# Four graph layers in one kernel: layernorm per block, and each layer's projections placed inside its first output block

## The chip, the cores and the metric

The kernel runs on one core of one Trainium2 chip. The metric is the device time of one execution in microseconds. Before the change three executions took 3187.55, 3188.2 and 3189.6 us; the median is 3188.2. The profiled execution has a span of 3186.7 us. Lower is better.

## The reference

There are N = 4096 nodes with D = 256 features, and a 0/1 matrix `adj` of 4096 x 4096 with ones on its diagonal. Four layers follow one another; each adds its result to the features and normalises every row to mean 0 and variance 1 (layernorm). So layer n+1 needs the normalised rows of layer n.

```python
x = _layernorm(x + _L0_gnn_ref(x, adj, W, a))          # additive attention, 4 heads of 64
x = _layernorm(x + _L1_gnn_ref(x, adj, Wq, bq, ...))   # multi-head attention, 4 heads of 64
x = _layernorm(x + _L2_gnn_ref(x, adj, W, a))          # additive attention, one head of 256
x = _layernorm(x + _L3_gnn_ref(x, adj, Wq, Wk))        # attention by cosines, 128 wide
```

- Layers 0 and 2: `Wh = x @ W`; the score of target i and source j is `leaky_relu(s_i + s_j)`, where both terms are products of `Wh` with a vector; where `adj` is 0 the weight is 0; softmax over the sources j; the output is the weighted sum of `Wh`, through `elu`.
- Layer 1: `q`, `k`, `v` are `x @ W + b`; the scores `q . k / 8` get a mask that takes away entries without an edge; softmax; weighted sum of `v`.
- Layer 3: `q` and `k` are `x @ Wq.T` and `x @ Wk.T`, with each row scaled to length 1; the score is their product; masked softmax; the result is `0.5 * (weighted sum of x) + 0.5 * x`. For a node with no neighbour at all the sum is replaced by x itself.

## The kernel before, in words

Rows are held in 32 tiles of 128 rows (`NT`); four of them (`QB`) make a block of 512 rows, so there are 8 blocks (`NB`). The features stay in one SBUF tensor `X` for the whole kernel, with a column of ones behind the 256 features.

Each layer has the same shape:

1. *A prologue over the 8 blocks.* `transposed_block` turns a block's tiles on TensorE (L92) and copies them to SBUF, one half on VectorE and one on ScalarE (L94 to L96). Then the projections: `additive_values` for layers 0 and 2 (L145, with three small exponentials on ScalarE and one multiply on VectorE for each tile, L147 to L152), keys, queries and values for layer 1 (L347 to L358), rows and their lengths for layer 3 (L496 to L507). Layer 1 then takes a maximum over all keys and queries for its shift (L361 to L374). Layer 3 takes a square root over all lengths, scales the rows (L513), turns them and copies them into `T` (L515 to L518). PSUM tiles of the prologue come in two buffers for each name.
2. *A loop over output blocks b and source tiles j.* `weights(b, j)` makes the masked, unnormalised softmax weights of 128 sources and 512 targets: an activation on ScalarE (L209, L402, L283, L536), then a multiply by the mask on VectorE (L210, L405, L285, L537). Masks are loaded in pieces through SyncE's queue, in layer 3 through GpSimd's. `sums(b, j)` adds the weighted features in PSUM on TensorE (L219 and L223, L425, L291, L544). `sums` is issued one step behind `weights` (two in layer 3). Layer 1 also makes its scores on TensorE (L400) and adds its denominators on GpSimd and by accumulating DMAs (L412, L418); its weights have 8 buffers.
3. *Outputs of block b - 1*, placed a few steps into block b: division by the denominator, `elu` in layers 0 and 2, the addition to `X`, and the mean and variance of each row (`row_stats`, L99).
4. *After the loop*, the outputs of the last block, and `layernorm` over all 32 tiles: one square root on ScalarE (L105), one reciprocal (L106) and 32 subtract-and-multiply operations on VectorE (L109). In layer 3 the results go to the DRAM in eight stores (L580).

In layer 0 the target term of each block must lie along the free dimension of all 128 partitions. `rows(b)` does this with one transpose and a way through DRAM (L192 to L200).

The code is written for a framework with a scheduler. It gives each engine one queue in an order of its own, from the order of the statements and from its idea of what is ready; an engine then works through its queue in order, and waits on semaphores. A buffer of a pool can be used again when its last readers have signalled. A pool that is opened where another was closed waits for the work in the old one.

Of the kernel before, what the change touches and what calls it, by code (L numbers as in the profile page):

```python
# [26 lines left out]
def kernel(  # L27
# [24 lines left out]

    nc = tc.nc
# [3 lines left out]

    const = ctx.enter_context(tc.tile_pool(name="const", bufs=1))
    feat = ctx.enter_context(tc.tile_pool(name="feat", bufs=1))

    ident = const.tile([P, P], FP, name="ident")
    make_identity(nc, ident)
    eps = const.tile([P, 1], FP, name="eps")
    nc.vector.memset(eps, EPS)


    X = feat.tile([P, NT, D + 1], FP, name="X")
    xv = x.rearrange("(t p) d -> p t d", p=P)
    for b in range(NB):
        nc.sync.dma_start(X[:, b * QB:(b + 1) * QB, :D], xv[:, b * QB:(b + 1) * QB, :])  # L70
    nc.vector.memset(X[:, :, D:], 1.0)
    stats = feat.tile([P, NT, 2], FP, name="stats")
    rstd = feat.tile([P, NT], FP, name="rstd")

    def load_w(pool, w, name):
        sb = pool.tile([P, KC, w.shape[1]], FP, name=name)
        nc.scalar.dma_start(sb, w.rearrange("(c p) f -> p c f", p=P))
        return sb

    def spread(pool, ap, dims, shape, name):  # L80

        sb = pool.tile(shape, FP, name=name)
        nc.scalar.dma_start(sb, bass.AP(tensor=ap.tensor, offset=ap.offset, ap=[[0, P]] + dims))
        return sb

    def transposed_block(sb, ps, b):

        xT = sb.tile([P, KC, QW], FP, name="xT")
        for c in range(KC):
            pt = ps.tile([P, QB, P], FP, name="px")  # L90
            for k in range(QB):
                nc.tensor.transpose(pt[:, k, :], X[:, b * QB + k, c * P:(c + 1) * P], ident)  # L92
            if c % 2:
                nc.scalar.copy(xT[:, c, :], pt.rearrange("p k i -> p (k i)"))  # L94
            else:
                nc.vector.tensor_copy(xT[:, c, :], pt.rearrange("p k i -> p (k i)"))  # L96
        return xT

    def row_stats(sb, y, t):  # L99
        st = sb.tile([P, 6], FP, name="bn")  # L100
        nc.vector.bn_stats(st, y)  # L101
        nc.vector.bn_aggr(stats[:, t, :], st)

    def finish_stats():
        nc.scalar.activation(rstd, stats[:, :, 1], AF.Sqrt, bias=eps)  # L105
        nc.vector.reciprocal(rstd, rstd)  # L106

    def normalise(y, t):
        nc.vector.tensor_scalar(y, y, stats[:, t, 0:1], rstd[:, t:t + 1], OP.subtract, OP.mult)  # L109

    def layernorm():
        finish_stats()
        for t in range(NT):
            normalise(X[:, t, :D], t)

# [4 lines left out]
    def additive_values(keep, w, a_src, a_dst, H, slope):  # L120

        d = D // H
        g = 1.0 - slope
        V = keep.tile([P, NT, D + H], FP, name="V")
        src = keep.tile([P, NT, H], FP, name="src")
        dst = keep.tile([P, NT, H], FP, name="dst")
        with tc.tile_pool(name="ga_w", bufs=1) as wp, \
             tc.tile_pool(name="ga_in", bufs=2) as sb, \
             tc.tile_pool(name="ga_ps", bufs=2, space=PSUM) as ps:
            w_sb = wp.tile([P, KC, D + 2 * H], FP, name="w_sb")  # L130
            nc.scalar.dma_start(w_sb[:, :, :D], w.rearrange("(c p) f -> p c f", p=P))
            for n, vec in enumerate((a_src, a_dst)):
                a_sb = spread(wp, *vec, [P, H, d], f"a{n}")
                for c in range(KC):
                    prod = sb.tile([P, H, d], FP, name="prod")
                    nc.vector.tensor_tensor(prod, w_sb[:, c, :D].rearrange("p (h d) -> p h d", h=H), a_sb, OP.mult)
                    lo = D + n * H
                    nc.vector.tensor_reduce(w_sb[:, c, lo:lo + H], prod, AX.X, OP.add)
            for b in range(NB):
                xT = transposed_block(sb, ps, b)  # L140
                for k in range(QB):
                    t = b * QB + k
                    pw = ps.tile([P, D + 2 * H], FP, name="pw")
                    for c in range(KC):
                        nc.tensor.matmul(pw, xT[:, c, k * P:(k + 1) * P], w_sb[:, c, :],  # L145
                                         start=(c == 0), stop=(c == KC - 1))
                    nc.scalar.activation(src[:, t, :], pw[:, D:D + H], AF.Exp, scale=g)  # L147
                    nc.scalar.activation(dst[:, t, :], pw[:, D + H:], AF.Exp, scale=g)
                    nc.scalar.activation(V[:, t, D:], pw[:, D + H:], AF.Exp, scale=slope)
                    nc.vector.tensor_tensor(V[:, t, :D].rearrange("p (h d) -> p h d", h=H),  # L150
                                            pw[:, :D].rearrange("p (h d) -> p h d", h=H),
                                            V[:, t, D:].unsqueeze(2).to_broadcast([P, H, d]), OP.mult)  # L152
        return V, src, dst

    def add_elu(sb, po, rden, t, H):

        o = sb.tile([P, D], FP, name="o")
        heads = "p (h d) -> p h d"
        nc.vector.tensor_tensor(o.rearrange(heads, h=H), po.rearrange(heads, h=H),
                                rden.unsqueeze(2).to_broadcast([P, H, D // H]), OP.mult)  # L160

        neg = sb.tile([P, D], FP, name="neg")
        nc.vector.tensor_scalar_min(neg, o, 0.0)
        nc.scalar.activation(neg, neg, AF.Exp)
        nc.vector.scalar_tensor_tensor(o, neg, -1.0, o, OP.add, OP.max)
        nc.vector.tensor_tensor(X[:, t, :D], X[:, t, :D], o, OP.add)
        row_stats(sb, X[:, t, :D], t)

    def additive_heads(w, a_src, a_dst, H, slope):
# [5 lines left out]
        MJ = 4  # L175
        with ExitStack() as lay:
            keep = lay.enter_context(tc.tile_pool(name="ga_keep", bufs=1))
            V, src, dst = additive_values(keep, w, a_src, a_dst, H, slope)
            rp = lay.enter_context(tc.tile_pool(name="ga_row", bufs=2))
            zp = lay.enter_context(tc.tile_pool(name="ga_z", bufs=5))  # L180
            sb = lay.enter_context(tc.tile_pool(name="ga_sb", bufs=2))
            mp = lay.enter_context(tc.tile_pool(name="ga_mask", bufs=3))
            dr = lay.enter_context(tc.tile_pool(name="ga_dram", bufs=2, space=bass.MemoryType.DRAM))
            ps = lay.enter_context(tc.tile_pool(name="ga_pr", bufs=1, space=PSUM))
            pa = lay.enter_context(tc.tile_pool(name="ga_pa", bufs=2, space=PSUM))
            edges = adjT.rearrange("(t p) i -> p t i", p=P)
            row, mask, acc, prob, kept = {}, {}, {}, {}, {}

            def rows(b):

                pr = ps.tile([QB * H, P], FP, name="pr")
                nc.tensor.transpose(pr, src[:, b * QB:(b + 1) * QB, :].rearrange("p k h -> p (k h)"), ident)  # L192
                line = sb.tile([QB * H, P], FP, name="line")
                nc.scalar.copy(line, pr)
# [18 lines left out]
            def sums(b, js):  # L213
# [11 lines left out]
                if js[-1] == NT - 1:  # L225
                    kept[b] = sb.tile([P, HC + 1, QW], FP, name="kept")
                    for c in range(HC + 1):
                        (nc.vector.tensor_copy if c == 1 else nc.scalar.copy)(kept[b][:, c, :], acc[b][:, c, :])

            def outputs(b, k):  # L230
                po = ps.tile([P, HC + 1, P], FP, name="po")
                for c in range(HC + 1):
                    nc.tensor.transpose(po[:, c, :], kept[b][:, c, k * P:(k + 1) * P], ident)
                rden = sb.tile([P, H], FP, name="rden")
                nc.vector.reciprocal(rden, po[:, HC, ::G])
                add_elu(sb, po[:, :HC, :].rearrange("p c f -> p (c f)"), rden, b * QB + k, H)

            rows(0)
            pairs = [(b, (j, j + 1)) for b in range(NB) for j in range(0, NT, 2)]
            for i in range(len(pairs) + 1):  # L240
                if i < len(pairs):
# [3 lines left out]
                    if js[0] == 2 and b + 1 < NB:  # L245
                        rows(b + 1)
                if i:
                    b, js = pairs[i - 1]
                    sums(b, js)
                    if b and js[0] % 6 == 2 and js[0] // 6 < QB:  # L250
                        outputs(b - 1, js[0] // 6)
            for k in range(QB):
                outputs(NB - 1, k)
            layernorm()

    def additive_one(w, a_src, a_dst, slope):

        MJ = 4
        with ExitStack() as lay:
            keep = lay.enter_context(tc.tile_pool(name="gb_keep", bufs=1))  # L260
            V, src, dst = additive_values(keep, w, a_src, a_dst, 1, slope)
            zp = lay.enter_context(tc.tile_pool(name="gb_z", bufs=3))
            sb = lay.enter_context(tc.tile_pool(name="gb_sb", bufs=2))
            mp = lay.enter_context(tc.tile_pool(name="gb_mask", bufs=3))
            edges = adjT.rearrange("(t p) i -> p t i", p=P)
            row = keep.tile([P, N], FP, name="row")
# [355 lines left out]
```

## Time and profile before

| engine | busy us | share of 3186.7 us |
|---|---|---|
| TensorE (matmul) | 3061.1 | 96% |
| VectorE | 1901.7 | 60% |
| ScalarE | 1661.7 | 52% |
| GpSimd | 825.6 | 26% |

The first product of each loop tells the stages apart: layer 0's loop starts at 72 us, layer 1's at 904, layer 2's at 1963 and layer 3's at 2503; the last products of the loops end at about 783, 1884, 2407 and 3164. A busy TensorE is not a TensorE at its peak, since matmuls are pipelined and their ends modelled; so the distance between repeated instructions is used as well as the busy time. The profile has eight loads of ScalarE's function tables, at 1283 ns each.

### The profile page before, as it was taken

How to read it: one execution, taken by the hardware profiler on the slowest of the kernel's cores; microseconds unless marked ns; L12 is line 12 of the kernel's file. 1: busy time of each engine (PE TensorE's matmuls, PEld its weight loads, DVE VectorE, ACT ScalarE, POOL GpSimd, SP SyncE). 2: the span in 40 equal slices, each digit the busy share in tenths (PEclk: the TensorE clock that was granted, in tenths of full speed). 3: DMA queues.
4: the chain of work that ended last, by engine and by line, in shares of the span. 5: the costliest groups of instructions: out<-in, count | busy, mean ns of one | idle time of the engine just before them, and what ended most of it. 6: DMA issues, size and time to landing. Idle time of an engine off the chain costs nothing. (4 is left out here: it accounts for less than half of the span.)

```text
span 3186.7 us, 37692 instructions
## 1 busy us (share of the span) xinstructions
PE 3061.1 (96%) x14220; PEld 1581.0 (50%) x14220; DVE 1901.7 (60%) x2594; ACT 1661.7 (52%) x2581; POOL 825.6 (26%) x534
## 2 busy tenths in 40 slices
PE   6999999998899999999999979999997999999997
PEld 4222222222543333333333327888886677777775
DVE  3899999998456666666666663454545333333333
ACT  3999999997245555555555543444443322222221
POOL 0000000000048878778778750000000000000000
PEclk9999999999999999999999989999998999999998
DMA  3323333321059989889889871444440433333331
GB/s 126 119 93 106 106 106 110 116 94 60 12 119 218 198 201 215 200 202 216 200 201 217 200 176 53 146 158 146 157 147 4 67 53 47 47 53 53 53 53 53
DMA packets 186263, 390.61 MB, mean 123 GB/s; under 512 B 10721, under 2 KB 53985, under 8 KB 185057
## 3 DMA queue, kind: packets, MB, share of 16 engines
q0 software_dynamic: 67840, 159.40, 27.5%
q1 hardware_dynamic: 114560, 226.58, 22.1%
q10 hardware_dynamic: 3680, 2.23, 0.2%
q8 instruction: 111, 1.82, 0.2%
q14 instruction: 72, 0.58, 0.1%
HBM read 283.25 MB, written 4.26 MB: 90 GB/s over the span
## 5 line engine op out<-in xcount | busy, mean ns | idle before, releaser
L405 DVE TENSOR_TENSOR prob<-p,mask 128x1024 f32<-128x1024 f32 x512 | 596.0, 1218 | 332.7 <-ACT p L402 249.0
L402 ACT ACTIVATE p<-p,shift 128x1024 f32<-128x1024 f32 x512 | 529.3, 1087 | 405.4 <-PE p L400 405.0
L209 ACT ACTIVATE prob<-row,dst 128x512 f32<-128x512 f32 x1024 | 645.4, 712 | 52.1 <-PE acc L223 47.3
L412 POOL TENSOR_TENSOR den<-den,prob 128x1024 f32<-128x1024 f32 x248 | 614.4, 2477 | 132.1 <-DVE prob L405 119.3
L210 DVE SCALAR_TENSOR_TENSOR prob<-prob,mask 128x2048 f32<-128x2048 f32 x256 | 586.5, 2291 | 73.8 <-ACT prob L209 69.1
L400 PE MATMUL p<-qT,kT 64*128 64x512 f32 x2048 | 496.3, 609 | 3.4 <-DVE prob L405 3.0
L544 PE MATMUL acc<-X,prob 128*128 128x257 f32 x2048 | 486.4, 381 | 3.5 <-DVE prob L537 3.5
L425 PE MATMUL acc<-prob,V 128*64 128x512 f32 x2048 | 480.2, 601 | 0.0
L219 PE MATMUL acc<-prob,V 128*64 128x512 f32 x2048 | 469.9, 601 | 8.3 <-DVE prob L210 8.3
L544 PEld LDWEIGHTS acc<-X,prob 128*128 128x128 f32 x2048 | 389.0, 191 | 164.9 <-issue 112.4
L291 PE MATMUL acc<-V,prob 128*128 128x257 f32 x2048 | 444.4, 380 | 0.9 <-ACT row L273 0.9
L537 DVE TENSOR_TENSOR prob<-prob,mask 128x512 f32<-128x512 f32 x256 | 176.3, 691 | 435.9 <-ACT prob L536 426.4
L536 ACT ACTIVATE prob<-p 128x512 f32<-128x512 f32 x256 | 152.4, 598 | 512.0 <-PE p L533 464.4
L291 PEld LDWEIGHTS acc<-V,prob 128*128 128x128 f32 x2048 | 388.6, 190 | 56.6 <-ACT row L273 1.2
L400 PEld LDWEIGHTS p<-qT,kT 64*128 64x128 f32 x2048 | 185.6, 187 | 309.1 <-DVE prob L405 168.3
L531 POOL DMA_DIRECT2D mask<-in_adjT x32 | 28.1, 880 | 1188.2 <-ACT kT L518 611.0
L283 ACT ACTIVATE e<-row,dst 128x512 f32<-128x512 f32 x256 | 185.2, 724 | 244.1 <-DVE prob L285 222.4
L285 DVE SCALAR_TENSOR_TENSOR prob<-e,mask 128x512 f32<-128x512 f32 x256 | 176.9, 691 | 222.3 <-PE acc L291 214.1
L219 PEld LDWEIGHTS acc<-prob,V 128*64 128x64 f32 x2048 | 136.2, 137 | 315.1 <-issue 222.6
L425 PEld LDWEIGHTS acc<-prob,V 128*64 128x64 f32 x2048 | 130.5, 136 | 324.1 <-issue 313.5
L533 PE MATMUL p<-kT,qT 128*128 128x512 f32 x512 | 259.6, 592 | 0.7 <-ACT kT L518 0.7
L223 PE MATMUL acc<-prob,V 128*32 128x512 f32 x2048 | 246.1, 598 | 0.0
(114 smaller groups left out, 1516.5 us busy)
## 6 DMA issues: line engine op xcount, KB each, us to landing
mask<-in_adjT SPq DMA_DIRECT2D x128, 1024.0 KB
den<-prob POOLq DMA_DIRECT2D x240, 512.0 KB, 5.7
mask<-in_adj SPq DMA_DIRECT2D x128, 512.0 KB
mask<-in_adjT POOLq DMA_DIRECT2D x32, 1024.0 KB, 8.2
row<-far SPq DMA_DIRECT2D x8, 1024.0 KB
den<-prob SPq DMA_DIRECT2D x16, 512.0 KB
X<-in_x SPq DMA_DIRECT2D x8, 512.0 KB
out<-Y SPq DMA_DIRECT2D x8, 512.0 KB
```

Of the source, the lines that this page charges most:

```text
L209: nc.scalar.activation(z[:, h, :], row[b][:, h, :], AF.Relu, bias=-1.0, scale=dst[:, j, h:h + 1])
L210: nc.vector.scalar_tensor_tensor(z, z, 1.0, mask[m][:, j % MJ, :].unsqueeze(1).to_broadcast([P, H, QW]), OP.add, OP.mult)
L219: nc.tensor.matmul(acc[b][lo:lo + d, h // 2, :], V[:, j, h * d:(h + 1) * d], prob[b, j][:, h, :], start=(j == 0), stop=(j == NT - 1))
L223: nc.tensor.matmul(acc[b][h * G:(h + 1) * G, HC, :], V[:, j, D + h:D + h + 1].to_broadcast([P, G]), prob[b, j][:, h, :], start=(j == 0), s ...
L291: nc.tensor.matmul(acc[b][k], prob[b, j][:, k * P:(k + 1) * P], V[:, j, :], start=(j == 0), stop=(j == NT - 1))
L400: nc.tensor.matmul(p[:, r, :], kT[half, c, j * P:(j + 1) * P], qT[half, c, cols], start=True, stop=True)
L402: nc.scalar.activation(p, p, AF.Exp, bias=shift)
L405: nc.vector.tensor_tensor(z, p, mask[m][:, j % MJ, :].unsqueeze(1).to_broadcast([P, KC, QW]), OP.mult)
L412: nc.gpsimd.tensor_tensor(to, to, flat, OP.add)
L425: nc.tensor.matmul(acc[b][r * d:(r + 1) * d, c, :], V[:, j, h * d:(h + 1) * d], prob[b, j, c][:, r, :], start=(j == 0), stop=(j == NT - 1))
L533: nc.tensor.matmul(p, T["q"][:, j * P:(j + 1) * P], T["k"][:, cols], start=True, stop=True)
L544: nc.tensor.matmul(acc[b][k], prob[u][:, k * P:(k + 1) * P], X[:, j, :], start=(j == 0), stop=(j == NT - 1))
```

## The change

The change is for the stretches between the loops, where a layer waits for the one before it.

- **Layernorm by block.** When the fourth tile of a block has its mean and variance, the block is normalised at once (`layernorm_block`), inside the loop. The inverse root is now `exp(-0.5 * ln(v))` with one Newton step on VectorE (`inverse_root`), in place of a square root and a reciprocal.
- **Projections inside the first block.** In layers 0, 2 and 3 a function `prepare(b)` does the transposes and projections of one block. Blocks 0 and 1 go ahead of the loop; blocks 2 to 7 are placed among the products of output block 0, one for each four source tiles. Layer 0's first row comes from 16 transposes of a broadcast column in place of the way through DRAM. Layer 3 makes its projections of queries and keys in one product of 256 columns, and its inverse lengths by `inverse_root` for each block.
- **The last block inside the next layer.** `additive_heads` and `multi_head_attention` return a function `tail`, which the next layer calls: layer 1 behind the keys of its block 0, layer 2 ahead of its loop. Layer 2's last outputs stand ahead of layer 3's `prepare(0)`.
- **Buffers.** PSUM tiles of all these are 512-column banks from one shared pool (`bank`): eight in layer 1's prologue, two in layer 0, four in layer 2 (shared with the sums of odd blocks), two in layer 3 (shared with the scores of later blocks). All pools release by tile. Layer 1's weights have 7 buffers instead of 8. The weights of layers 0, 1 and 2 are loaded at the start.
- **Layer 3's outputs** leave out the case of a node without neighbours (no row lacks its diagonal), and are stored by block.

```diff
+    def inverse_root(v, n):
+        r = fin.tile([P, n], FP, name=f"r{n}")
+        nc.scalar.activation(r, v, AF.Ln)
+        nc.scalar.activation(r, r, AF.Exp, scale=-0.5)
...
+        nc.vector.tensor_tensor(s, r, r, OP.mult)
+        nc.vector.tensor_tensor(s, s, v, OP.mult)
+        nc.vector.tensor_scalar(s, s, -0.5, 1.5, OP.mult, OP.add)
+        nc.vector.tensor_tensor(r, r, s, OP.mult)
+        return r
...
+    def normalise(ys, mv):
...
+        nc.vector.tensor_scalar_add(v, mv[:, :, 1], EPS)
+        r = inverse_root(v, n)
+        for k, y in enumerate(ys):
+            nc.vector.tensor_scalar(y, y, mv[:, k, 0:1], r[:, k:k + 1], OP.subtract, OP.mult)
...
-            rows(0)
+            prepare(0)
+            first_rows()
+            prepare(1)
...
+                    if b == 0 and js[0] % QB == 2 and js[0] // QB + 2 < NB:
+                        prepare(js[0] // QB + 2)
...
-            for k in range(QB):
-                outputs(NB - 1, k)
-            layernorm()
...
+        def tail(bank):
             for k in range(QB):
-                outputs(NB - 1, k)
-            layernorm()
+                outputs(bank, NB - 1, k)
+        return tail
...
-                 tc.tile_pool(name="mh_ps", bufs=2, space=PSUM) as ps:
+                ps = pool(pro, "mh_ps", 8, space=PSUM)
...
+                keys(0)
+                tail(bank)
+                values(0)
...
-            zp = lay.enter_context(tc.tile_pool(name="mh_z", bufs=8))
+            zp = pool(lay, "mh_z", 7)
...
-                nc.scalar.activation(norm, norm, AF.Sqrt)
-                nc.vector.tensor_scalar_max(norm, norm, 1e-4)
-                nc.vector.reciprocal(norm, norm)
...
+                nc.vector.tensor_scalar_max(v, norm.rearrange("p k n -> p (k n)"), 1e-8)
+                r = inverse_root(v, QB * 2)
+                flat = rows.rearrange("p k n f -> p (k n) f")
+                nc.vector.tensor_tensor(flat, flat, r.unsqueeze(2).to_broadcast([P, QB * 2, P]), OP.mult)
...
+            prepare(0)
+            prepare(1)
             units = [(b, j) for b in range(NB) for j in range(NT)]
...
+                    if b == 0 and j % QB == 2 and j // QB + 2 < NB:
+                        prepare(j // QB + 2)
```

## The prediction

> **What bounds the kernel now.** I read, in this order, the busy time by stage (windows I cut where the traced layers change), the chain of work that ended last, the costliest groups, and the instructions in order of time around the seams. Columns of the first view: window, its length, then busy us (and instructions) of TensorE (PE), its weight loads (PEld), VectorE (DVE), ScalarE (ACT) and GpSimd (POOL), then granted clock, DMA share, GB/s.
>
> ```profile
> 0.00:72.00 72.00, 44.26 (x199) 32.79 (x199) 23.64 (x51) 21.64 (x118) 0.70 (x6) 0.94 0.41 139
> 72.00:783.00 711.00, 711.00 (x4175) 198.30 (x4179) 640.11 (x458) 653.49 (x1063) 0.00 (x0) 1.00 0.32 102
> 783.00:904.00 121.00, 101.40 (x351) 58.36 (x340) 59.13 (x139) 31.18 (x48) 0.00 (x0) 0.92 0.03 9
> 904.00:1884.00 980.00, 976.08 (x4266) 328.08 (x4266) 628.50 (x595) 543.14 (x535) 796.79 (x496) 1.00 0.91 204
> 1884.00:1963.00 79.00, 51.88 (x248) 37.25 (x246) 38.26 (x95) 24.13 (x121) 0.00 (x0) 0.85 0.17 52
> 1963.00:2407.00 444.00, 443.95 (x2047) 388.56 (x2048) 222.08 (x453) 192.18 (x281) 0.00 (x0) 1.00 0.46 145
> 2407.00:2503.00 96.00, 71.26 (x399) 53.71 (x398) 54.60 (x198) 43.75 (x163) 2.70 (x3) 0.88 0.10 15
> 2503.00:3164.00 661.00, 661.00 (x2548) 483.93 (x2548) 219.04 (x544) 151.86 (x254) 25.43 (x29) 1.00 0.32 49
> 3164.00:3186.70 22.70, 0.24 (x2) 0.00 (x0) 16.31 (x66) 0.32 (x1) 0.00 (x0) 0.61 0.56 185
> ```
>
> The four loops (711, 980, 444, 661 us) are TensorE's; the five seams between and around them sum to 72 + 121 + 79 + 96 + 22.7 = 391 us, of which TensorE works 269. Only the seams can shrink, and their matrix work does not vanish: it moves into a loop that TensorE already bounds.
>
> The chain says the same:
>
> ```profile
> 1963.05 443.09 PE acc L291 x2042
> 2414.70 6.61 DVE X L109 x21
> ...
> 2497.53 4.70 issue
> ...
> 3170.42 6.87 DVE Y L109 x21
> ```
>
> Layer 2's loop is one unbroken run of products; around it, the normalisation of all 32 tiles (L109) and a wait for the first mask (4.7 us) are bare time.
>
> Layer 0's loop matters for added work, because there the other engines are nearly full too:
>
> ```profile
> L209 ACT ACTIVATE prob<-row,dst 128x512 f32<-128x512 f32 x1024 | 645.4, 712 | 52.1 <-PE acc L223 47.3
> L210 DVE SCALAR_TENSOR_TENSOR prob<-prob,mask 128x2048 f32<-128x2048 f32 x256 | 586.5, 2291 | 73.8 <-ACT prob L209 69.1
> ```
>
> A pair of source tiles takes 5.44 us on TensorE (products start at 433.61, the next pair's transposes at 439.04). ScalarE needs 8 x 645.4/1024 = 5.04 us of it, VectorE 2 x 2.29 = 4.58.
>
> **What the Trainium skill says.** "ScalarE: Activation LUTs", section "What ACT_TABLE_LOAD costs": a switch of table set is about 1283 ns plus a drain of about 1380 ns. The trace agrees with the first and shows no drain of that size:
>
> ```profile
> 2493.40 0.59 ACT L518 COPY kT<-px 128x512 f32<-128x512 f32 x1 [0.20 <-PE px L517]
> 2494.01 1.28 ACT L536 ACT_TABLE_LOAD   x1
> 2495.30 0.60 ACT L536 ACTIVATE prob<-p 128x512 f32<-128x512 f32 x1
> ```
>
> The load starts 0.02 us after the copy ends, and the exponential starts as it ends, so I take 1.28. Same page, section "Table sets: the hidden batching unit": Ln and Exp share one set and need one load. The instruction order of the built program disagrees for this change: it has a load before each Ln and another before the Exp after it, 83 in all against 8. "TensorE: Matmul & The Clock Gate", section "What's actually happening": after some 3.4 us idle the matrix clock falls to half. The granted clock agrees (1.00 in loops, 0.85 to 0.92 in seams); fewer gaps help a little, which I do not count.
>
> **Part by part.** A 512-column fp32 pass takes 2.59/6 = 0.432 us (layer 3's unit of six such passes repeats every 2.59 us), a 257-column one 443.09/2048 = 0.216.
>
> *Start, layer 0.* Seam 72 us: input loads to 13, eight blocks' projections to 59, then 13 for the first row's way through DRAM. After: two blocks, and the first row by transposes. Loads again 13 (the attention vectors of layer 2 are now attached first on VectorE, 8 operations of about 0.41, partly behind their loads); block 0 projected by 18; row by 21; first tile's four Relus 2.5 and mask 2.3: first products at 26. Block 1 leaves 3 us. Six blocks remain inside: eight transposes 1.04, 16 projection passes 3.5, one head pass left without its partner 0.86, some seven switches of array shape at (5.44 - 12 x 0.432)/2 = 0.13, waits 0.7: 7 us each, 42. Sum 71: gain 1. The order places each copy and projection between mask operations, so ScalarE (10.1 + 2 per two pairs, against TensorE's 10.9 + 7) is not the bound.
>
> *Layer 0 to 1.* Seam 121. Projections cannot enter the loop (the shift needs all maxima), so eight blocks remain: 1.04 + 16 x 0.432 + 16 x 0.216 = 11.4 each, 91. Measured is 12.1 (97 us from 807 to 904), with two PSUM buffers per name instead of eight shared. Add 2 to start, 1.5 for the tail's transposes, 3 for VectorE being behind: 97.5. Gain 24: the 13 us of outputs and the wait for normalised tiles lie beside projections.
>
> *Layer 1 to 2.* Seam 79. After: block 0's projection to the first mask, 8; block 1 to 12; tail's sums and transposes 3; six blocks inside at 1.04 + 16 x 0.217 + 0.45 = 5, with switches 6: 36. Sum 51, gain 28. ScalarE and VectorE have over half their time free here (192 and 222 of 444).
>
> *Layer 2 to 3.* Seam 96. Block 0 waits on one chain: copies behind the last block's outputs on VectorE, projections 3.5, squares, Ln and Exp with loads 3, but ScalarE's order puts the last layernorm's pair, another 3, before the block's T copies; scaling 1.23, transposes, copies, scores, mask: first products at 23. Block 1 leaves 3.5. Six inside: 1.04 + 3.45 + 1.04 = 5.5 of TensorE, plus a stall: the order leaves 4.3 us of other products between the last projection and the transposes of the scaled rows, and squares 0.8, an exponential 0.6, Ln and Exp 3, small operations 0.75, scaling 1.23, signals 0.5 need 6.9. I take 2.6; bounds 0 (all hidden) and 6.9 (nothing). 6 x 8.1 = 49. Sum 76, gain 20.
>
> *End.* 22.7 to about 15: two tiles' outputs 3.2, Ln and Exp 2 after a load begun early, the second pair 3.5, normalising 0.9, the store 5.5 (now from 3181 to the end). Gain 8.
>
> *Layernorm in the loops.* 7 blocks per layer; each puts two loads and two tiny activations, 2 x 1.28 + 0.4 = 3 us, in ScalarE's queue, and VectorE waits in order for the root with the mask products queued behind it, for which TensorE waits. Layer 0: tiles are ready only 0.9 to 1.5 us ahead (mask done at 426.69 and 429.15, products begin at 428.17 and about 430.0), ScalarE regains 0.4 per pair, and VectorE gets 2.5 more: I take 2.7 lost; bounds 0 and 5.5. 19. Layer 1: ScalarE pauses 2.4 us in each group of 5.50, so 1 lost; 7. Layers 2 and 3 run two tiles ahead (3.4 and 5.2 us): 0.5 each; 7. Sum 33. Layer 1's probability buffers go from 8 to 7: a buffer returns within about 10 us (accumulating DMA lands 5.7 after issue) and seven last 12.8, so nothing, bound 20.
>
> Net: 1 + 24 + 28 + 20 + 8 - 33 = 48 less; with 4 us from the higher clock and layer 1's removed start-up table load, 3188 - 52 = 3136.
>
> **Rivals.** *All of it hides*: no layernorm stall, no stall on the rows, 3136 - 33 - 16 = 3087. For: ScalarE waits 405 us in layer 1 and 464 in layer 3 for TensorE. Against: in-order queues and layer 0's lead of about 1 us. *New waits eat it*: layernorm 5.5 per block in layers 0 and 1 (77, 51 more than taken), rows 6.9 (26 more), layer 1 short of a buffer (20): 3136 + 97 = 3233, slower. For: 75 loads, 96 us of ScalarE, which nothing in the old trace shows inside a loop. Against: outside layer 0, ScalarE is at most 55% busy. *Half of that*, 3175: hardly worth it.
>
> **How the numbers follow.** Forecast 0.62, all hidden 0.20, half the waits 0.11, slower 0.07. The range reaches most of the way to both neighbours: 3092 to 3174. Faster by over 0.2% (below 3182): 0.90; within: 0.03; slower: 0.07.
>
> **What would show it.** Right: first products of layer 0 at 26 us and its loop end near 802; layer 1's projections starting within 3 us of layer 0's last product; 83 table loads of 1.28; TensorE waiting for masks once per block in layer 0; row transposes of layer 3 waiting 2 to 3 us on VectorE. Wrong: layer 1's groups longer than 5.50, or layer 0's two pairs with a projection above 18 us.

## The result, and the profile after

The changed kernel takes 3148.2 us (3145.2 to 3148.8), the kernel before 3188.7; the ratio is 0.9871, with a 95% interval of 0.9854 to 0.9888. So it is faster by 40 us. TensorE's idle time fell from 125.6 to 75.8 us, and its busy time rose by 10.2. The forecast was 3136: the sign and the size are right, and 12 us are missing. They are a small rest of errors that are larger and of both signs, so that the closeness of the sum is in part luck; these errors are what this part is about.

The first view is again the busy time by stage, now cut where the traced products of the changed kernel begin and end (same columns: window, length, TensorE, its weight loads, VectorE, ScalarE, GpSimd, granted clock, DMA share, GB/s).

```profile
0.00:31.60 31.60, 14.16 (x57) 10.09 (x57) 13.56 (x29) 9.02 (x28) 0.70 (x6) 1.00 0.89 293
31.60:783.40 751.80, 751.80 (x4340) 222.75 (x4341) 667.69 (x555) 679.69 (x1182) 0.00 (x0) 1.00 0.30 98
783.40:891.50 108.10, 98.30 (x340) 58.96 (x338) 48.16 (x101) 32.39 (x50) 0.00 (x0) 0.95 0.00 1
891.50:1890.30 998.80, 993.60 (x4266) 329.08 (x4265) 646.66 (x667) 563.25 (x562) 799.02 (x496) 1.00 0.90 200
1890.30:1903.70 13.40, 12.84 (x71) 8.93 (x69) 6.70 (x13) 8.10 (x34) 0.00 (x0) 1.00 0.91 275
1903.70:2385.70 482.00, 478.16 (x2232) 413.93 (x2231) 255.46 (x570) 228.16 (x397) 0.00 (x0) 1.00 0.42 134
2385.70:2411.10 25.40, 15.02 (x63) 10.88 (x62) 14.55 (x47) 15.58 (x47) 2.70 (x3) 0.80 0.77 125
2411.10:3134.80 723.70, 707.36 (x2755) 516.30 (x2753) 249.83 (x524) 218.88 (x430) 25.36 (x29) 0.99 0.29 48
3134.80:3147.10 12.30, 0.03 (x1) 0.00 (x0) 6.49 (x30) 4.66 (x7) 0.00 (x0) 0.68 0.13 43
```

Beside the prediction's terms, put together by stage (for instance layer 0's loop: 711 + 3 + 42 + 19), this gives:

| stage | before | forecast | after | after less forecast |
|---|---|---|---|---|
| start to layer 0's first product | 72 | 26 | 31.6 | +5.6 |
| layer 0's loop | 711 | 775 | 751.8 | -23.2 |
| layer 0 to 1 | 121 | 97.5 | 108.1 | +10.6 |
| layer 1's loop | 980 | 987 | 998.8 | +11.8 |
| layer 1 to 2 | 79 | 15 | 13.4 | -1.6 |
| layer 2's loop | 444 | 483.5 | 482.0 | -1.5 |
| layer 2 to 3 | 96 | 26.5 | 25.4 | -1.1 |
| layer 3's loop | 661 | 713.5 | 723.7 | +10.2 |
| end | 22.7 | 15 | 12.3 | -2.7 |
| clock and start-up load | | -4 | in the rows above | +4 |

The sum of the last column is 12.1. Four rows carry most of it: layer 0's loop came out 23 us better, and the step from layer 0 to 1, layer 1's loop and layer 3's loop each 10 to 12 us worse.

Second, the groups of the changed kernel that answer to the two of layer 0 shown before, and the table loads:

```profile
L238 ACT ACTIVATE prob<-row,dst 128x512 f32<-128x512 f32 x1024 | 644.1, 709 | 52.0 <-PE acc L252 47.6 <-issue 3.5 <-ACT V L155 0.8
L119 ACT ACT_TABLE_LOAD x41 | 52.6, 1283 | 0.8
L120 ACT ACT_TABLE_LOAD x40 | 51.3, 1283 | 0.7
```

ScalarE's Relus take as long as before and wait for TensorE as much as before (47.6 us), although the root of each block now needs two loads of 1.28 us in its queue (81 of the 83 in the whole run, 14 of them in layer 0's loop). Third, what TensorE waits for, in the whole run (us in all, times, longest):

```profile
PE g L616 <- DVE rows L612: 16.3, 7, 2.4
PE g L409 <- DVE xT L108: 6.4, 7, 3.1
PE acc L248 <- DVE prob L239: 0.2, 1, 0.2
```

Layer 0's products (L248) wait once for a mask, 0.2 us: its seven layernorms cost nothing. Layer 3's row transposes (L616) wait seven times for the scaled rows, 16.3 us. What the waits don't show is the clock behind them, nor layer 1, where TensorE counts as busy for 993.6 us and still needs 19 us more than before.

### The profile page after: what moved, and what is told of

The parts are those of the page before. It is cut to its first block, busy times and chain, and to the rows that moved or that the text cites. A ratio compares the mean times of both kernels' runs of the same rounds, so it can differ in the third digit from the quotient of the medians.

```text
span 3147.1 us, 37355 instructions
## 1 busy us (share of the span) xinstructions
PE 3071.3 (98%) x14107; PEld 1570.9 (50%) x14107; DVE 1909.1 (61%) x2530; ACT 1759.7 (56%) x2734; POOL 827.8 (26%) x534
## 4 chain that ended last, share of the span: by engine, by line
PE 89%; DVE 6%; ACT 3%; issue 1%; DMA 0%; SPq 0%; DVEq 0%; ACTq 0%
PE acc L248 15%; PE p L474 14%; PE acc L499 14%; PE acc L635 14%; PE acc L252 8%; PE acc L343 5%; PE g L343 5%; PE p L625 4%; PE g L625 3%; PE g L409 2%; PE g L151 2%; DVE prob L337 1%; ACT L120 1%; PE g L601 1%; PE g L421 1%
## 5 line engine op out<-in xcount | busy, mean ns | idle before, releaser
L238 ACT ACTIVATE prob<-row,dst 128x512 f32<-128x512 f32 x1024 | 644.1, 709 | 52.0 <-PE acc L252 47.6
L486 POOL TENSOR_TENSOR den<-den,prob 128x1024 f32<-128x1024 f32 x248 | 624.2, 2517 | 121.7 <-DVE prob L479 109.7
L474 PE MATMUL p<-qT,kT 64*128 64x512 f32 x2048 | 506.6, 609 | 4.5 <-DVE prob L479 3.9
L635 PE MATMUL acc<-X,prob 128*128 128x257 f32 x2048 | 492.2, 383 | 0.0
L499 PE MATMUL acc<-prob,V 128*64 128x512 f32 x2048 | 487.7, 601 | 0.7 <-ACT kept L504 0.7
L248 PE MATMUL acc<-prob,V 128*64 128x512 f32 x2048 | 476.5, 599 | 0.2 <-DVE prob L239 0.2
L635 PEld LDWEIGHTS acc<-X,prob 128*128 128x128 f32 x2048 | 389.6, 191 | 164.1 <-issue 116.7
L499 PEld LDWEIGHTS acc<-prob,V 128*64 128x64 f32 x2048 | 131.8, 136 | 327.2 <-issue 315.0
L248 PEld LDWEIGHTS acc<-prob,V 128*64 128x64 f32 x2048 | 136.4, 136 | 300.8 <-issue 223.3
L484 POOL COPY den<-prob 128x1024 f32<-128x1024 f32 x8 | 8.8, 1101 | 896.0 <-DVE prob L479 895.9
L492 POOL DMA_DIRECT2D den<-prob x240 | 222.9, 929 | 71.8 <-DVE prob L479 46.6
L343 PE MATMUL acc<-V,prob 128*128 128x257 f32 x1024 | 225.8, 380 | 0.9 <-DVE prob L337 0.9
L343 PE MATMUL g<-V,prob 128*128 128x257 f32 x1024 | 223.8, 380 | 1.2 <-DVE prob L337 1.2
```

The source lines that it names most:

```text
L238: nc.scalar.activation(z[:, h, :], row[b][:, h, :], AF.Relu, bias=-1.0, scale=dst[:, j, h:h + 1])
L248: nc.tensor.matmul(acc[b][lo:lo + d, h // 2, :], V[:, j, h * d:(h + 1) * d], prob[b, j][:, h, :], start=(j == 0), stop=(j == NT - 1))
L343: nc.tensor.matmul(acc[b][k][:, :D + 1], prob[b, j][:, k * P:(k + 1) * P], V[:, j, :], start=(j == 0), stop=(j == NT - 1))
L474: nc.tensor.matmul(p[:, r, :], kT[half, c, j * P:(j + 1) * P], qT[half, c, cols], start=True, stop=True)
L486: nc.gpsimd.tensor_tensor(to, to, flat, OP.add)
L492: nc.gpsimd.dma_start(to, flat, accum_op=OP.add)
```

## The experiments

Eleven kernels were run; each was timed beside the kernel before. Times are medians; stage lengths are from each kernel's trace, cut as above.

**One table set.** The Trainium skill, "ScalarE: Activation LUTs", section "Table sets: the hidden batching unit", names a set that holds both Ln and Exp; the program as built takes another set for each. The edit asks for that set by name:

```diff
+    nc.scalar.preload_act_table_set("natural_log_exp_and_others")
```

> The changed kernel with one added line: the table set that holds both the logarithm and the exponential is loaded once at the start, so that 82 of the 83 table loads fall away and nothing else changes. Theory A (loads are hidden in layers 0 to 2 and cost on the path only in layer 3's in-loop preparation, where they make the rows late by 2.1 to 2.4 us and the clock falls after): the seven waits, 16.3 us, and five spells of half clock at 1.7 each, 8.5, vanish; layer 1 gains 0.7 per block, 5; the step from layer 2 to 3 and the end 2.6 each: 35 less, 3113 us (3108 to 3120), and layer 0's loop stays within 1 us of 752. Theory B (the prediction's prices: every layernorm costs TensorE time, 2.7 a block in layer 0): 33 for the layernorms and 16 for the rows, 49 less, 3099, with layer 0's loop about 19 shorter. Theory C (the load is not what makes the rows late): within 5 us of 3148.

Measured: 3110.0 us, ratio 0.9755 (0.9741 to 0.9770), one table load in the trace. The loops, in order of the layers:

```profile
34.40:786.20 751.80, 751.80 (x4340) 222.76 (x4340) 665.58 (x555) 665.06 (x1168) 0.00 (x0) 1.00 0.31 98
891.30:1888.00 996.70, 992.42 (x4266) 329.46 (x4266) 651.67 (x667) 544.90 (x548) 799.40 (x496) 1.00 0.90 201
1901.30:2377.70 476.40, 476.40 (x2232) 414.66 (x2231) 256.29 (x570) 208.50 (x381) 0.00 (x0) 1.00 0.43 136
2398.60:3098.30 699.70, 699.04 (x2755) 510.36 (x2753) 250.28 (x524) 182.62 (x401) 25.36 (x29) 1.00 0.30 49
```

Layer 0's loop is 751.8 us with its loads and without them. Layer 3's loses 24.0, layer 2's 5.6, layer 1's 2.1, the step from 2 to 3 4.5, the end 2.5. Two other stages moved as well: the start is 2.8 longer, where the operations of layer 2's vectors stand elsewhere in VectorE's queue and the first of them starts behind its load at 20.1 us, not at 16.3; the step from 0 to 1 is 3.0 shorter, with 3.4 us of half clock in it and not 10.2. Theory A holds in place and sum, except that it gave layer 2 nothing and layer 1 5; B falls with layer 0, C with the sum.

**Layer 3's row transposes later, loads kept.**

```diff
-                        prepare(j // QB + 2)
+                        due[i + 3] = j // QB + 2, prepare(j // QB + 2)
...
+                    if i in due:
+                        turn(*due[i])
```

`turn` holds the row transposes and their copies into `T`, which `prepare` no longer does.

> The changed kernel with all its table loads; in layer 3 only, the transposes of a block's scaled rows are put three tiles after its projections in the program, so that 7.8 us of other products lie between them and not 4.3. Theory A (the chain from projection to scaled rows is 6.8 us long, and only its length against the work placed in between counts): the waits of the six in-loop blocks go, some 14 us, and the five spells of half clock with them, 8.5: 22 less, 3126 us (3122 to 3132), granted clock 1.00 in layer 3's loop. Theory B (ScalarE's time for the loads is what is short, so that the wait moves to the exponentials of the next tiles): at most 5 less, 3143 to 3150, TensorE waiting elsewhere in the same loop.

Measured: 3128.0 us, ratio 0.9808 (0.9792 to 0.9824). Layer 3's loop falls from 723.7 to 704.3; of the seven waits two are left:

```profile
PE g L619 <- DVE rows L612: 4.5, 2, 2.4
```

One of these is block 1's, whose transposes the edit does not move behind three tiles; the other is block 2's, whose transposes stand in the same place of TensorE's queue as without the edit. Theory A. So what made the rows late is the length of the chain, loads included, against the work placed beside it; ScalarE has the time for the loads. The two edits also show what a late row costs: 11.8 us of waits went in the one (16.3 less 4.5), 15.6 in the other (0.7 are left), and the loop lost 19.4 and 24.0. The rest is the clock. In the changed kernel's timeline (start, length, engine, operation, idle time before it and what ended it):

```profile
2483.40 1.03 PE L635 MATMUL acc<-X,prob 128*128 128x257 f32 x4
2486.86 1.59 PE L616 MATMUL g<-ident,rows 128*128 128x128 f32 x8 [2.43 <-DVE rows L612]
2488.24 1.92 PE L635 MATMUL acc<-X,prob 128*128 128x257 f32 x4
```

The same four products (L635) take 1.03 us ahead of the wait and 1.92 behind it. The granted clock was halved for 3.41 us behind five of the seven waits, which costs 1.7 each, 8.5 in all: 15.6 + 8.5 is the 24 that one table set gained there, and 11.8 with four of the five spells, 6.8, is nearly the 19.4 of this edit.

**Layer 0's layernorm made longer.** In the in-loop layernorms of layer 0 alone:

```diff
         nc.scalar.activation(r, r, AF.Exp, scale=-0.5)
+        if twice:
+            nc.scalar.activation(r, r, AF.Ln)
+            nc.scalar.activation(r, r, AF.Exp)
```

> The changed kernel with the root of layer 0's seven in-loop layernorms taken through two more activations (logarithm and exponential once more, which give the same value): two more table loads, 3.0 us more of ScalarE per block and, with the two Relus that the order puts between them, the root 4.4 us later for VectorE. Theory A (probability tiles are ready 4.4 and 3.0 us ahead in layer 0, the first layernorm uses all but 0.5 us of it, which is why it is free): the second costs 2.5 to 3.9 us per block, 17 to 27 in all, 3165 to 3175 us, with layer 0's loop 17 to 27 longer than 752 and TensorE waiting for masks seven times. Theory B (layer 0 has far more slack than a layernorm needs): within 4 us of 3148. Theory C (the prediction's lead of 1 us, at which the first layernorm would already have cost 2.7): the whole 3.0 to 4.4 per block, 21 to 31.

Measured: 3182.8 us, the median of 20 executions between 3180.4 and 3189.2; ratio 0.9984 (0.9977 to 0.9991). The traced one took 3187.0, and layer 0's loop is 791.2 in it, 39.4 longer. The waits of TensorE are as A has them, 3.3 us each, seven times (the eighth is the first product); the time is far more:

```profile
430.22 3.68 PE L251 MATMUL acc<-prob,V 128*64 128x512 f32 x8 [3.30 <-DVE prob L242]
433.83 3.08 PE L255 MATMUL acc<-prob,V 128*32 128x512 f32 x16
436.84 3.65 PE L251 MATMUL acc<-prob,V 128*64 128x512 f32 x16
```

Eight products take 3.68 us behind the wait, and sixteen take 3.65 a little later. The trace has half clock for 34.1 us in this loop: 17.1 us lost, and 23.1 of waits, are 40.2. A is right on the slack and left out the clock, so that its 3165 to 3175 us were too few; B falls. C, whose first layernorm already costs, falls with the 751.8 above.

**Preparation ahead of the loops in layers 0 and 2.**

```diff
-            prepare(1)
+            for b in range(1, NB): prepare(b)
...
-                    if b == 0 and js[0] % QB == 2 and js[0] // QB + 2 < NB:
-                        prepare(js[0] // QB + 2)
```

(the same in layer 2, and the first product of each loop is queued behind the last projection).

> The changed kernel with one part undone in layers 0 and 2: the preparation of all blocks comes ahead of the first product, not among the first output block's products; blocks are still normalised one by one and the last block is still finished inside the next layer. Theory A (TensorE bounds both the preparation and the loop, so its matrix work costs the same in either place): layer 0 7 blocks at 5.75 ahead against 40.8 inside, layer 2 6 blocks at 5.6 ahead against 38 inside: 3143 to 3155 us. Theory B (the seams' gain came from placing the preparation inside the loops): most of what layer 0's and layer 2's seams shrank comes back, 40 and 28 us: 3180 to 3216.

Measured: 3151.3 us (3148.2 to 3156.6), ratio 0.9884 (0.9869 to 0.9899), so 3 us more than the changed kernel, within the spread of these executions. Start and loop of layer 0 take 73.8 + 710.9 = 784.7 against 783.4; the step from 1 to 2 and layer 2's loop 51.6 + 448.9 = 500.5 against 495.4. Theory A: placing projections inside a loop that TensorE bounds gives almost nothing. In the kernel before, the step from 1 to 2 and layer 2's loop took 523; so 22.6 of the 27.7 us gained there come from what this edit leaves in, and that is that nothing waits any more for the layernorm of all tiles and the last block. For layer 0 the whole change gained about 1 us, as forecast: before, its last product ended at 784.3.

**Layer 1: outputs in one piece.** TensorE's order around a block's outputs, in the changed kernel (first line: a run of products elsewhere, up to 1040.19):

```profile
1037.46 2.79 PE L499 MATMUL acc<-prob,V 128*64 128x512 f32 x12
...
1406.05 0.66 PE L525 MATMUL p<-ident,kept 128*128 128x128 f32 x4
1406.63 1.07 PE L499 MATMUL acc<-prob,V 128*64 128x512 f32 x2
1407.63 0.66 PE L518 MATMUL p<-ident,kept 128*128 128x128 f32 x4
1408.22 1.93 PE L499 MATMUL acc<-prob,V 128*64 128x512 f32 x6
```

Two products (L499; the profile counts two for each head) take from 1406.63 to 1407.63, 1.0 us; elsewhere twelve take 2.73, or 0.46 for two. Two heads use half of TensorE's array each, and these times show them side by side when they follow each other: a pair takes 0.91 us, and some 1.1 more when it is split. The Trainium skill, "TensorE: Matmul & The Clock Gate", section "Part 3: Packing small matmuls — row/col tiling", says that small matmuls at different places in the array run concurrently. Here a transpose came between the two. Counted over the loop, 21 pairs are split in the changed kernel, 12 of them by a transpose; in the kernel before 7 are, none by a transpose. The edit gives all of layer 1's TensorE instructions one order by hand:

```diff
+        def queue(i):
+            if line and line[0] is not None:
+                tc.add_manual_dep(i.ins, line[0].name, ...)
...
+                            queue(nc.tensor.transpose(pos[-1][:, i, c * P:(c + 1) * P], ...))
```

> The changed kernel with TensorE's order in layer 1's loop fixed: a block's denominators, its eight output transposes and the transposes of the denominators run in one piece between two tiles, so that no transpose lies between the two half-array products of a pair (heads r = 0 and r = 1), as it does two or three times per block now. Theory A (a pair that is split runs one after the other, 0.5 us more each, and every switch between shapes costs 0.1): 2.2 us per block over seven blocks, 15 less, 3133 us (3129 to 3138), with layer 1's loop at 984 against 999. Theory B (the extra 3 us per block are the layernorm's: loads on ScalarE and the normalising on VectorE ahead of the masks): within 3 us of 3148.

Measured: 3152.8 us, ratio 0.9887 (0.9872 to 0.9902); layer 1's loop 1005.7. Neither theory: no pair is split any more, score products are 12 us shorter (506.6 to 494.4), and these waits came in:

```profile
PE p L480 <- DVE prob L485: 17.9, 10, 3.1
PE acc L505 <- ACT kept L510: 8.4, 10, 1.0
```

Behind five of the waits for masks TensorE runs at half clock for 3.41 us, which costs 8.5 us more.

**Both edits together.** The same order, with one table set.

> Both edits together: one table set for the whole kernel, and layer 1's outputs in one piece between two tiles. With the pieces alone layer 1's loop took 1005.7 us, TensorE's score products being 12 us shorter and 14 us of new waits for masks in their place; with one set alone 996.7. Theory A (two causes stand behind each other: the split pairs hide the wait that the layernorm's loads make, so neither edit alone gains and both together do): loop of layer 1 at 983 to 989, 3110 - 10 = 3100 us (3096 to 3104). Theory B (what delays the masks is VectorE's own order, with statistics and normalising put ahead of them, and not ScalarE's loads): loop at 998 or more, 3110 to 3115 us.

Measured: 3112.8 us, ratio 0.9763 (0.9748 to 0.9778); layer 1's loop 998.3. Theory B: without the loads the waits for masks are still 13.3 us, and three spells of half clock cost 5.1 more. Theory B's reason is VectorE's own order: a block's statistics, root and normalising are put ahead of the masks for which the scores' buffers wait. The runs with the layernorm in VectorE's gaps, further down, test it.

**Two small waits.** The attach of layer 2's vectors goes behind block 1's projections, and layer 1's transposes one block ahead:

```diff
+            last = prepare(1)
+            with tc.issue_after(last): early2()
...
                     keys(b)
+                    turned(b + 1)
```

> One table set, and two small waits taken out: layer 2's attention vectors are attached on VectorE after block 1's projection, not before block 0's transposed copy; in layer 1 a block's transposes come ahead of the values of the block before. Theory A (both waits are bare time of TensorE): the first product of layer 0 at 29 to 30 us, not at 34.4, 5 less; seven waits of 0.6 us and one of 3.1 in the step from layer 0 to 1 gone, 105.1 to 99, 6 less; 3110 - 11 = 3099 us (3096 to 3104). Theory B (each wait gives way to the next one behind it, the copies of the rows in layer 0, the biases and maxima in layer 1): within 4 us of 3110.

Measured: 3097.6 us, ratio 0.9715 (0.9699 to 0.9731). Start 27.5, layer 0's loop 2.2 longer, the step from 0 to 1 95.8, the step from 2 to 3 1.1 longer: 12.5 us less in all, theory A.

**Layernorm in VectorE's gaps.** Layer 1's layernorm in four steps, one per group of three tiles, each behind the group's third mask, without and with the outputs in one piece:

```diff
+                    if todo:
+                        with tc.issue_after(masked[0]):
+                            todo.pop(0)()
...
-                                close(u[0] - 1)
+                                todo.extend(steps(u[0] - 1))
```

> The kernel with one table set and the two small waits taken out (3097.6 us, layer 1's loop 996.9), and in layer 1 the layernorm of a finished block cut into four steps (statistics of two tiles, of two more, the root, the normalising), each put on VectorE behind the third mask of a group, where VectorE idles 1.95 us. Theory A (split pairs and the layernorm's place on VectorE stand behind each other: taking away one leaves the other): 0.4 to 0.7 us per block, loop 992 to 997, 3093 to 3098 us. Theory B (the layernorm's place is the whole of it): loop 982 to 986, 3083 to 3087.

Measured: 3102.5 us, ratio 0.9729 (0.9715 to 0.9744); layer 1's loop 1002.0, so slower than expected of either.

> The same, and with layer 1's outputs in one piece between two tiles as well. Theory A (both causes together are what layer 1's loop lost against the kernel before, 980): loop 979 to 985, 3097.6 - 15 = 3083 us (3080 to 3087). Theory B (the loop is held by a third thing, such as the probability buffers, seven where there were eight, or VectorE waiting for GpSimd's additions): loop 992 or more, 3093 us or more.

Measured: 3088.7 us, ratio 0.9684 (0.9668 to 0.9700); loop 987.4, a little short of theory A's range. Layer 1's loop in the kernel before and in the four with one table set; the one with no split pair and the layernorm when ready lacks the two small waits' edit, which moved this loop by 0.2 us only (waits are the loop less TensorE's busy time):

| pairs split | layernorm | TensorE busy | of it lost to half clock | waits | loop |
|---|---|---|---|---|---|
| 7 (kernel before) | after the loop | 976.1 | 1.7 | 3.9 | 980 |
| 21 | when ready | 992.7 | 0 | 4.2 | 996.9 |
| 21 | in the gaps | 994.6 | 0 | 7.4 | 1002.0 |
| 0 | when ready | 975.2 | 5.1 | 23.1 | 998.3 |
| 0 | in the gaps | 971.4 | 0 | 16.0 | 987.4 |

Neither edit alone gains, both together win 9.5: two causes, each of which hides the other's removal. In the gaps, joining the 21 pairs takes 23.1 us off TensorE's busy time, 1.1 each, and 8.6 come back as waits, nearly all for the copies of finished sums (0.7 to 8.4). With the layernorm when ready the waits for masks (3.2 to 13.3) and the half clock behind them take the rest as well. Why the gaps alone cost 5 was not tried by itself. Their trace shows waits for masks of 6.7 us where there were 3.2, and slower normalising on VectorE: its 28 operations take 28.6 us, not 11.4 (the last section says why).

**The waits at block ends.** The same, with the order left free where a block ends.

> All of the last kernel (one table set, two small waits out, layernorm steps in VectorE's gaps, outputs in one piece), with TensorE's order in layer 1 left free where an output block ends, so that the next block's scores fill the ten waits of 0.7 to 1.0 us for the copies of the finished sums, 8.4 us. Theory A (those waits are bare): 3 to 6 us less, 3083 to 3086. Theory B (filling them splits a pair at each block's end and gives as much back): within 2 us of 3088.7.

Measured: 3087.2 us, ratio 0.9681 (0.9666 to 0.9695), loop 986.9. Theory B: the waits for the copies fall from 8.4 to 0.7 us and the loop by 0.5. The trace has seven split pairs again, one for each block end, and 7.2 us more of busy TensorE. This version is 2% faster than the changed kernel; its 1.5 us against the one before are no more than the spread of the executions.

**All loads kept, only the order changed.**

> The changed kernel with all 83 table loads, and only the order of work changed: layer 3's row transposes three tiles later, layer 1's outputs in one piece with the layernorm's steps in VectorE's gaps, the two small waits taken out. Theory A (where a load falls counts, and not how many there are): what 82 loads still cost is what one set gained outside layer 3's rows and layer 1, 5.6 in layer 2, 4.5 in the step from 2 to 3, 2.5 at the end, and one row wait left in layer 3, 4.6: 3088.7 + 17 = 3106 us (3101 to 3111), layer 1's loop within 3 us of 987. Theory B (loads in layer 1 delay the exponentials wherever they stand): layer 1's loop above 995, 3112 us or more.

Measured: 3113.5 us, ratio 0.9763 (0.9747 to 0.9780). Layer 1's loop is 993.8: between the theories, loads cost 6.4 there. Against the same order with one set (3088.7 us; layer 3's rows differ in place) 82 loads, 105 us of ScalarE, cost 25 us; in the changed kernel as it stood they cost 38.

## Why the prediction was right in sum and wrong in its parts

- *Start, 26.* Measured 31.6. The attach of layer 2's vectors was taken as 8 operations "partly behind their loads". It is the wait for the load that counts: the first of these operations stands ahead of block 0's copy in VectorE's queue, and the chain that ended last goes through its load. With the attach moved (and one table set), the first product came at 27.5, not at 34.4.

```profile
11.00 5.25 DMA a<-in_a
17.87 6.27 PE g L151 x16
```

- *Six prepares inside at 7 us each.* Two pairs with a projection start 17.0 us apart (69.96, 86.96; the bound was 18), so one costs 17.0 - 2 x 5.44 = 6.1.
- *Layernorm in layer 0, 2.7 per block, 19 in all: the step that failed most.* The prediction read a lead of "only 0.9 to 1.5 us" by pairing each product with the mask that ended last before it. In the kernel before:

```profile
421.42 2.29 DVE L210 SCALAR_TENSOR_TENSOR prob<-prob,mask 128x2048 f32<-128x2048 f32 x1 [0.17 <-ACT prob L209]
424.40 2.29 DVE L210 SCALAR_TENSOR_TENSOR prob<-prob,mask 128x2048 f32<-128x2048 f32 x1 [0.69 <-ACT prob L209]
426.86 2.29 DVE L210 SCALAR_TENSOR_TENSOR prob<-prob,mask 128x2048 f32<-128x2048 f32 x1 [0.17 <-ACT prob L209]
427.24 1.34 ACT L209 ACTIVATE prob<-row,dst 128x512 f32<-128x512 f32 x2 [0.41 <-PE acc L223]
428.17 3.65 PE L219 MATMUL acc<-prob,V 128*64 128x512 f32 x16
```

There are five probability buffers, and ScalarE starts tile k + 5 as tile k's products end (427.24); so the mask that ends at 429.15 is that of tile k + 4, and the pair whose products start at 428.17, k + 2 and k + 3, had its masks at 423.71 and 426.69. The leads are 4.5 and 3.3 us (the second tile's products begin at about 430.0), and a layernorm fits in; the run with a longer root shows that little more would have. "TensorE waiting for masks once per block" did not come, and the cost was nothing, not 19.
- *Layer 0 to 1, 97.5.* The eight blocks take 12.0 us each (816.87 to 828.90), the old kernel's 12.1 and not the 11.4 taken, because each waits 0.6 for its copy: 4.8 in all. The one wait of 3.1 for a copy behind the last block's outputs on VectorE was in the forecast. Left out was the clock, halved for 6.8 us behind this wait and for 3.4 behind one for a maximum, which costs 5.1. With one table set, moving the transposes took 9.3 away.
- *Layer 1's loop, 7 for the layernorm.* Groups stay at 5.50, as said, and no wait for one of the seven buffers shows. But the change also cut the outputs into halves, whose transposes land between the halves of a pair: 14 more pairs are split than before, some 15 of the 18.8 us by which the loop grew. The prediction looked for waits and did not price the new order of TensorE itself. Split pairs and the layernorm's place on VectorE stand behind each other here, and both had to go before the loop moved.
- *Layers 1 to 2 and 2 to 3, and layer 2's loop.* Within 2 us.
- *Layer 3's rows, a stall of 2.6.* The mechanism is right, and the wait is 2.3 on average (16.3 / 7). The term left out is the clock: the prediction named the falling clock, and counted only a gain from it. The loop's excess of 62.7 is 16.3 of waits, 8.5 of half clock and, as the rest, 37.9 of products; with one table set, where 0.7 of the waits and none of the half clock are left, it is 38.7.
- *The gain.* The prediction said that the matrix work of the seams only moves. That is what the run with the preparation ahead shows: 1.3 and 5.1 us for the two layers.

Open: where layer 2's 5.6 us with loads come from (3.8 of them are waits that the trace shows), and whether layer 1's loop could come back to 980. In the run with 987.4 TensorE is busy 4.7 us less than in the kernel before and waits 12.1 more: of its waits 8.4 are for copies of finished sums, 6.2 for masks and 1.4 for outputs.

## What to carry to other kernels

Price an added operation by the lead of what it delays, and find the lead by counting buffers, not by taking the neighbour in time. When work is put among the products of an engine that is the bound, look at what it comes between: a pair that runs side by side, or a chain that is longer than the work placed in it. Where an edit gains nothing, a second cause may be standing behind the first; change both before dropping either.

## What the runs showed of the hardware

- *Short waits halve TensorE's clock.* The Trainium skill, "TensorE: Matmul & The Clock Gate", section "What's actually happening", has the clock fall after about 3.4 us without work, in a window that runs on its own. Here waits of 2.1 to 2.4 us were enough, in five of seven cases in layer 3; of the seven waits of 3.30 us in the run with a longer root one cost nothing more, and half clock followed for 3.41 us twice and for 6.83 us four times. The traces show why. In each of them the spells start a whole number of 3.413 us apart, the length that the page gives for the window (in layer 3 at 2432.63, 2449.70 and 2487.24: 5 and 11 of them). When the time is cut on this grid of starts, a stretch in which TensorE idled 2.09 us or more was followed by half clock in these fourteen cases, and one with 1.71 or less was not: the wait from 2484.43 to 2486.86 lies in one stretch, the one from 2465.67 to 2468.10 is cut into 1.09 and 1.34. The clock stayed down for a second stretch where 0.79 us or more of the first was idle, and came back at 0.56 or less. In all thirteen traces, behind the first loads, 2.05 us or more was always enough and less than 1.27 never; between these both happened.
- *A small VectorE operation can wait for GpSimd.* The first step of the root in layer 1, with one table set, on 4 elements per partition (minimum, median, maximum in ns), and below it the same in layer 0, where GpSimd is idle:

```profile
L122 DVE TENSOR_TENSOR s<-r x7: 161/1415/1725, 1041.0 to 1792.9; 128x4 f32<-128x4 f32 x7
```

```profile
L122 DVE TENSOR_TENSOR s<-r x7: 155/156/158, 236.6 to 771.1; 128x4 f32<-128x4 f32 x7
```

In layer 1 five of the seven start while GpSimd adds, and end 0.02 to 0.03 us after its addition (in the last block GpSimd adds from 1791.95 for 2.34 us, and the operation ends at 1794.31); the two others, of 161 and 162 ns, meet no addition. The Trainium skill, "GPSIMD Engine Reference", section "1. Specifications", says that GpSimd shares its SBUF interfaces with VectorE, and contends with operations of two SBUF inputs; this is one. The masks, with one input in PSUM, keep to 1.22 us beside the same additions. In the gaps the normalising is hit too: in each block one of the four operations on 256 columns, of 0.40 us otherwise, takes 1.61 to 3.31 us and ends some 0.16 after an addition (from 1423.51 to 1426.81; GpSimd adds until 1426.65).
